# LayerNorm outputs transposed once in float32 instead of twice in split form, in a fused attention and ternary feed-forward kernel

## The chip, the cores and the metric

The kernel runs on one core of a Trainium2 chip. The metric is the device time of one execution in microseconds (us). Before the change it is 1569.74 us, the median of three runs (1567.95 to 1573.29).

The engines are named as in the profile: PE (TensorE, matrix multiplication; PEld are its weight loads), DVE (VectorE), ACT (ScalarE), POOL (GpSimd) and SP (SyncE, which here only issues DMAs). Each engine works through its own queue in order and waits on semaphores for the others.

## The reference

The input x has 8 batches of 1024 tokens with 256 features. The reference is a sandwich of two sublayers, each with a LayerNorm (without weights) ahead of it and one behind it:

```python
x = x + _layernorm(_L0_attn_ref(_layernorm(x), Wq, Wk, Wv, Wo))
x = x + _layernorm(_L0_ffn_ref(_layernorm(x), weight, alpha, bias))
```

```python
q, k, v = x @ Wq, x @ Wk, x @ Wv      # 16 query heads, 4 key/value heads of 16
q, k = _rope(q), _rope(k)
p = softmax(einsum('bhqd,bhkd->bhqk', q, k) / sqrt(256))
o = einsum('bhqk,bhkd->bhqd', p, v)
return o @ Wo
...
w = ternary_quantize(weight) * alpha   # entries -1, 0, 1
return einsum('bsd,od->bso', input, w) + bias
```

All of it is float32.

## The kernel before

**Tiling.** The tokens are cut into 16 units of 512 (`NU`), two per batch; a unit is four tiles of 128 tokens, handled as two pairs p = 0 and 1. For each unit there are three streams of work.

- The *projection* (class `Project`): LayerNorm of x (`begin`), transposing the normalised pairs so that features lie on the partitions (`x`), key/value product (`kv_and_dram`, then `kt` and `v`), query product (`q`), and the way of the queries through DRAM into the stacked layout `q_st` (`q_to_dram`, `stack_queries`).
- The *attention scores*: PE computes scores twice. The first time (`sm`, line 608) DVE takes row maxima (line 621). The maxima go through a small transpose (`pm`, line 655) and a DMA (`q_st<-ml`, line 671) into extra rows of the queries, so that the second scores (`se`, line 680) come out shifted and ACT can take the exponential directly (line 701). The exponentials are multiplied by the values (`av`, line 721), and `av_out` sends the sums to DRAM (`d_av<-avsb`, line 742).
- The *tail* (class `Tail`): fetch of the sums, division by the softmax denominator, output product `attn`, LayerNorm and residual (`stats_a`), second LayerNorm (`stats_x`), transposing (`x` or `xw`), ternary product `ffn`, last LayerNorm and residual (`stats_f`), store.

**Split products.** A product in full float32 is made from fp32r parts: each operand is split into a high part (rounded to fp32r) and a low part (the rest), and `product` (line 297) adds up high x high, high x low and low x high. Where an operand has to be transposed first, there are two ways in the kernel before:

- `transposed` (line 262) is called once for the high part and once for the low part. Both parts were made before, by POOL (`split_hi`, line 155: a multiplication by one that writes fp32r; `split_lo`, line 161: a subtraction). Each call is four 128x128 fp32r transposes on PE into one bank of PSUM and one copy by ACT (line 271).
- `transposed_split` (line 274) transposes the float32 values themselves, four 128x128 fp32 transposes into one bank (line 279). ACT copies the bank to SBUF once (line 284), and POOL makes both parts from that copy. Only the tails of units 12, 13 and 14 use it (`W_PARTS`, line 999, step name `xw`).

In the projections of units 3 to 15 the high and low parts `xs` take the buffer named `hl` in the pool `qkp`, which has one buffer; the split queries `hlq`, which four DMAs read, take the same one.

**Order.** A unit has 32 steps (`SPU`); a step is four exponent scores. `P_PARTS`, `T_PARTS` and their variants for the first and last units say at which step each part falls due; a projection starts at step 26 of one unit and ends at step 62, which is step 30 of the next; a tail runs during the unit after its own. On PE, ACT and DVE the order is written out (`manual_schedule`); for POOL and SP the recording layer orders the instructions. From exponent score 40 on the written order comes from a planner (`plan`, `Course`, `group`): it searches over *groups*, each of some `se` and `sm` scores, then parts that are due, then a piece of `av`. PSUM banks limit it: exponent scores and parts share three banks (`ps_e`), so a group holds three exponent scores and no part that needs a bank, or two and one such part. The planner works with costs on PE and ACT, in ns, in `WORK` (line 1199), and `banked` (line 1098) lists which parts need a bank.

Of the kernel before, what the change touches and what calls it, by code (L numbers as in the profile page):

```python
# [8 lines left out]
F32 = mybir.dt.float32  # L9
F32R = mybir.dt.float32r  # L10
# [6 lines left out]
P = 128  # L17
# [11 lines left out]
def kernel(  # L29
# [29 lines left out]
    nc = tc.nc  # L59
# [4 lines left out]
    ND = D // P  # L64
    NK = S // P
    UPB = S // UQ
    NU = B * UPB
# [8 lines left out]
    work = ctx.enter_context(tc.tile_pool(name="work", bufs=2))  # L76
# [78 lines left out]
    def split_hi(eng, hi, src):  # L155
        if eng is nc.gpsimd:
            eng.tensor_scalar(hi, src, 1.0, 0.0, ALU.mult, ALU.add)  # L157
        else:
            nc.scalar.copy(hi, src)

    def split_lo(eng, lo, src, hi):
        eng.tensor_tensor(lo, src, hi.bitcast(F32), ALU.subtract)  # L162

    def split(eng, hi, lo, src, hi_eng=None):

        split_hi(hi_eng or eng, hi, src)
        split_lo(eng, lo, src, hi)
# [25 lines left out]
    ffn = {}  # L193
# [68 lines left out]
    def transposed(src, tag, name, copy=nc.scalar.copy):  # L262

        pt = psum([P, ND, 2 * P], f"pt_{name}", F32R)
        for t in range(2):
            for c in range(ND):
                nc.tensor.transpose(  # L267
                    pt[:, c, t * P : (t + 1) * P], src[:, t, c * P : (c + 1) * P], ident_r
                )
        dst = work.tile([P, ND, 2 * P], F32R, tag=tag, name=name, bufs=2 if tag[0] == "x" else 1)  # L270
        copy(dst, pt.bitcast(F32))
        return dst

    def transposed_split(src, tag, name):

        pt = psum([P, ND, 2 * P], f"pt_{name}")
        for t in range(2):
            for c in range(ND):
                nc.tensor.transpose(
                    pt[:, c, t * P : (t + 1) * P], src[:, t, c * P : (c + 1) * P], ident  # L280
                )

        whole = work.tile([P, ND, 2 * P], F32R, tag="xt0", name=name).bitcast(F32)
        nc.scalar.copy(whole, pt)
        parts = [
            work.tile([P, ND, 2 * P], F32R, tag=f"{tag}{l}", name=f"{name}_{l}", bufs=1)
            for l in range(2)
        ]
        split(nc.gpsimd, *parts, whole)
        return parts  # L290

    TERMS = ((0, 0), (0, 1), (1, 0))
# [30 lines left out]
    class Project:  # L323
# [3 lines left out]
        def __init__(self, u, eng):  # L327
            self.u, self.eng = u, eng
            self.b, self.half = divmod(u, UPB)
            self.xt, self.sc, self.hl = {}, {}, {}  # L330
            self.q_rot = None
            if u not in (1, 2):
                xn = qkp.tile([P, UT, D], F32, tag="xn", name=f"xn_{u}", bufs=2)
                xs = qkp.tile([P, 2, UT, D], F32R, tag="hl", name=f"xs_{u}")
                self.xn = [xn[:, 2 * p : 2 * p + 2, :] for p in range(2)]
                self.xs = [[xs[:, l, 2 * p : 2 * p + 2, :] for l in range(2)] for p in range(2)]
            else:
# [21 lines left out]
        def begin(self, p):  # L359
            self.stats(p)  # L360
            self.norm(p)
            self.hi(p)
            self.lo(p)

        def x(self, p, l):
            self.xt[p, l] = transposed(self.xs[p][l], f"xt{l}", f"xt{l}_{self.u}_{p}")

        def kv(self, p):

# [375 lines left out]
    class Tail:  # L745
# [65 lines left out]
                self.copy(p)(hl[:, 0], self.on[p])  # L811
            split_lo(self.eng(p), hl[:, 1], self.on[p], hl[:, 0])

        def x(self, p, l):
            self.xt[p, l] = transposed(self.hl[p][:, l], f"ot{l}", f"ot{l}_{self.u}_{p}")

        def xw(self, p):
            self.xt[p, 0], self.xt[p, 1] = transposed_split(self.on[p], "ot", f"ot_{self.u}_{p}")

# [20 lines left out]
        def stats_x(self, p):  # L840
            self.sc[p] = ln_stats(self.x1[p])
            self.norm(p)
            if not NU - 4 <= self.u < NU - 1:
                self.split(p)

        def stats_f(self, p):
# [25 lines left out]
    class LastTail(Tail):  # L872
# [55 lines left out]
        x = o  # L928
# [42 lines left out]
    def load(u):  # L971
# [2 lines left out]


    P_PARTS = (
        (26, "begin", 0), (33, "x", 0, 0), (34, "x", 0, 1), (37, "begin", 1), (43, "x", 1, 0),
        (45, "x", 1, 1), (49, "kv_and_dram"), (51, "q", 0), (54, "kt"), (53, "v"), (55, "q", 1),
        (62, "q_to_dram"),
    )  # L980
    L_PARTS = (
# [5 lines left out]
    T_PARTS = (  # L987
        (1, "fetch"), (7, "invert"), (8, "scale", 0), (9, "scale", 1), (12, "attn", 0),
        (15, "attn", 1), (15, "stats_a", 0), (17, "stats_a", 1), (19, "stats_x", 0),
        (23, "stats_x", 1), (24, "x", 0, 0), (25, "x", 0, 1), (26, "ffn", 0), (27, "x", 1, 0),  # L990
        (29, "x", 1, 1), (31, "ffn", 1), (31, "stats_f", 0), (33, "stats_f", 1),
    )


    P_SECOND = (26, 33, 34, 37, 43, 45, 49, 51, 52, 53, 55, 57)
    T_FIRST = (6, 8, 11, 12, 14, 16, 16, 17, 20, 23, 24, 25, 26, 27, 29, 31, 31, 33)
    P_FIRST = (47, 51, 52, 54, 57, 58, 59, 60, 62, 61, 63, 64)

    W_PARTS = (
        (1, "fetch"), (7, "invert"), (8, "scale", 0), (9, "scale", 1), (12, "attn", 0),  # L1000
        (15, "attn", 1), (15, "stats_a", 0), (17, "stats_a", 1), (19, "stats_x", 0),
        (22, "xw", 0), (23, "stats_x", 1), (26, "ffn", 0), (27, "xw", 1), (31, "ffn", 1),
        (31, "stats_f", 0), (33, "stats_f", 1),
    )
    T_LAST = (1, 3, 4, 5, 9, 10, 11, 14, 17, 19, 20, 22, 25, 27, 24, 28)

    warm = []
# [76 lines left out]
    for u in range(NU - 1):  # L1084
        start = SPU * (u + 1)
        at(start + 1, begin_tail, u)
        parts = T_PARTS if u < NU - 4 else W_PARTS
# [82 lines left out]
    def window(s):  # L1170
# [26 lines left out]


    WORK = {
        "x": (460, 477), "xw": (460, 477), "q": (1620, 477), "kv_and_dram": (1620, 477),  # L1200
        "v": (330, 270), "attn": (1620, 477), "ffn": (1125, 560), "n": (460, 477),
        "o": (460, 477),
    }
# [345 lines left out]
```

## Time and profile before

| what | value |
|---|---|
| median of 3 runs | 1569.74 us |
| the profiled execution | 1569.75 us |
| its span, first to last instruction | 1568.0 us |
| mean granted PE clock | 0.996 |
| fp32r transposes, lines 267 (`pt_xt`, `pt_ot`) | 480 |
| fp32 transposes, line 279 (`pt_ot`) | 24 |
| ACT copies behind them, lines 271 and 284 | 118 + 6, mean 592 to 614 ns |
| POOL, high part of a pair, line 157 (`xs`, `hl`, `ot`) | 87, mean 619 to 623 ns |
| POOL, low part of a pair, line 162 (`xs`, `hl`, `ot`) | 89, mean 1273 to 1285 ns |
| DVE row maxima, line 621 | 605 of 128x1024 (1219 ns), 838 of 128x512 (683 ns) |

In a group line a name left of the arrow is what is written and names right of it are what is read; shapes are partitions by elements. The counts of lines 157 and 162 hold the splits of the attention output (`hl` in `scale`) too. A PE instruction's duration overlaps that of its neighbours, because matmuls are pipelined; its cost to the queue is read from the start of one piece of work to the start of the next.

### The profile page before, as it was taken

How to read it: one execution, taken by the hardware profiler on the slowest of the kernel's cores; microseconds unless marked ns; L12 is line 12 of the kernel's file. 1: busy time of each engine (PE TensorE's matmuls, PEld its weight loads, DVE VectorE, ACT ScalarE, POOL GpSimd, SP SyncE). 2: the span in 40 equal slices, each digit the busy share in tenths (PEclk: the TensorE clock that was granted, in tenths of full speed). 3: DMA queues.
4: the chain of work that ended last, by engine and by line, in shares of the span. 5: the costliest groups of instructions: out<-in, count | busy, mean ns of one | idle time of the engine just before them, and what ended most of it. 6: DMA issues, size and time to landing. Idle time of an engine off the chain costs nothing.

```text
span 1568.0 us, 35573 instructions
## 1 busy us (share of the span) xinstructions
PE 1527.8 (97%) x13854; PEld 779.0 (50%) x13854; DVE 1411.6 (90%) x2172; ACT 1268.8 (81%) x2473; POOL 835.8 (53%) x1239
## 2 busy tenths in 40 slices
PE   8999999999999999999999999999999999999997
PEld 6544454554545455454544545455454544444444
DVE  7888898999899999999999899999999999999965
ACT  4677878888887888888888888888888787878874
POOL 6553466383845647474573756547385543323354
PEclk9999999999999999999999999999999999999999
DMA  5161525133161513415152251514225151321100
GB/s 145 55 96 49 112 73 112 63 82 83 61 130 46 97 61 87 96 59 117 54 93 70 78 107 59 113 49 88 63 68 110 45 99 45 61 58 36 43 15 27
DMA packets 86071, 117.86 MB, mean 75 GB/s; under 512 B 12088, under 2 KB 50808, under 8 KB 85752
## 3 DMA queue, kind: packets, MB, share of 16 engines
q1 hardware_dynamic: 85904, 115.60, 31.9%
q8 instruction: 109, 1.79, 0.5%
q14 instruction: 58, 0.48, 0.1%
HBM read 68.65 MB, written 45.88 MB: 73 GB/s over the span
## 4 chain that ended last, share of the span: by engine, by line
PE 88%; DVE 5%; POOL 2%; DMA 2%; ACT 1%; issue 1%; SPq 0%; POOLq 0%; ACTq 0%; DVEq 0%
PE av L721 32%; PE se L680 27%; PE sm L608 13%; DVE mx L621 4%; PE pa L301 3%; PE pq L301 3%; PE pf L301 2%; PE pt_xt L267 2%; PE pt_ot L267 2%; PE pkv L301 1%; DMA q_st<-ml 1%; ACT e L701 1%; PE pm L655 1%; POOL lnsc L242 0%; DMA x<-in_L_attn_x 0%
## 5 line engine op out<-in xcount | busy, mean ns | idle before, releaser
L621 DVE TENSOR_REDUCE mx<-sm 128x1 f32<-128x512 f32 (+1 forms) x1443 | 1237.4, 908 | 112.7 <-PE sm L608 78.9
L701 ACT ACTIVATE e<-se 128x512 f32<-128x512 f32 x1996 | 1059.4, 600 | 161.5 <-PE sm L608 96.2
L608 PE MATMUL sm<-k_st,q_st 64*128 64x512 f32 x2048 | 692.1, 445 | 6.4 <-DVE mx L621 5.9
L680 PE MATMUL se<-q_st,k_st 64*128 64x512 f32 x2048 | 685.5, 439 | 9.9 <-DMA q_st<-ml 3.8
L721 PE MATMUL av<-e,v_aug 128*32 128x128 f32 (+3 forms) x7736 | 604.3, 402 | 0.0
L680 PEld LDWEIGHTS se<-q_st,k_st 64*128 64x128 f32 x2048 | 322.0, 184 | 421.4 <-ACT e L701 326.7
L608 PEld LDWEIGHTS sm<-k_st,q_st 64*128 64x128 f32 x2048 | 315.4, 184 | 40.6 <-DVE mx L621 24.1
L721 PEld LDWEIGHTS av<-e,v_aug 128*32 128x32 f32 x7736 | 167.6, 108 | 191.2 <-issue 143.5
L241 POOL TENSOR_SCALAR lnsc<-mv 128x2 f32<-128x2 f32 (+1 forms) x134 | 25.7, 192 | 355.5 <-DVE mv L239 349.8
L795 POOL TENSOR_TENSOR xn<-xn,a 128x512 f32<-128x512 f32 x30 | 38.4, 1281 | 124.4 <-DMA a<-d_rec 104.9
L242 POOL TENSOR_TENSOR lnsc<-lnsc,mhalf 128x2 f32<-128x2 f32 (+1 forms) x134 | 92.3, 689 | 0.9
L162 POOL TENSOR_TENSOR hl<-xn,hl 128x512 fp32r<-128x512 f32 x54 | 68.7, 1285 | 0.0
L253 POOL TENSOR_SCALAR xn<-x,lnsc 128x256 f32<-128x256 f32 x116 | 64.9, 568 | 3.4
L860 POOL TENSOR_TENSOR a<-a,bias_bc 128x512 f32<-128x512 f32 x30 | 38.4, 1282 | 45.8 <-ACT a L859 45.8
L157 POOL TENSOR_SCALAR xs<-xn 128x512 fp32r<-128x512 f32 x27 | 16.8, 623 | 68.2 <-DMA dq<-hlq 66.9
L301 PE MATMUL pq<-xt,wqkvh 128*128 128x256 f32 x256 | 44.1, 294 | 3.9 <-DVE ml L664 3.5
L315 POOL TENSOR_TENSOR t<-q_rot,sin_q_sb 128x512 f32<-128x512 f32 x31 | 40.2, 1298 | 12.6 <-ACT q_rot L457 11.6
L301 PE MATMUL pa<-woh,hl 128*128 128x256 f32 x240 | 46.3, 295 | 0.0
L237 DVE BATCH_NORM_STATS2 bnst<-x 128x6 f32<-128x256 f32 x124 | 45.8, 410 | 0.1
L237 DVE BATCH_NORM_STATS2 bnst<-a 128x6 f32<-128x256 f32 x120 | 44.6, 413 | 0.1
L301 PE MATMUL pf<-wt,ot 128*128 128x256 f32 x256 | 38.6, 292 | 5.2 <-ACT e L701 5.2
L825 ACT COPY a<-pa 128x512 f32<-128x512 f32 x30 | 17.6, 587 | 29.2 <-issue 29.2
(163 smaller groups left out, 1316.2 us busy)
## 6 DMA issues: line engine op xcount, KB each, us to landing
q_st<-dq SPq DMA_DIRECT2D x90, 256.0 KB
dq<-hlq SPq DMA_DIRECT2D x60, 256.0 KB
d_av<-avsb SPq DMA_DIRECT2D x60, 256.0 KB
x<-in_L_attn_x SPq DMA_DIRECT2D x15, 512.0 KB
xn<-d_av SPq DMA_DIRECT2D x30, 256.0 KB
a<-d_rec SPq DMA_DIRECT2D x30, 256.0 KB
xr<-in_L_attn_x SPq DMA_DIRECT2D x15, 512.0 KB
out_x<-a SPq DMA_DIRECT2D x30, 256.0 KB
```

Of the source, the lines that this page charges most:

```text
L162: eng.tensor_tensor(lo, src, hi.bitcast(F32), ALU.subtract)
L237: nc.vector.bn_stats(st[:, t, :], src[:, t, :])
L242: nc.gpsimd.tensor_tensor(sc[:, 1, :], sc[:, 1, :], mhalf[:, :n], ALU.pow)
L253: eng.tensor_scalar(dst[:, t, :], src[:, t, :], sc[:, 0, t : t + 1] if eng is nc.gpsimd else mv[:, t, 0:1], sc[:, 1, t : t + 1], ALU.add i ...
L267: nc.tensor.transpose(pt[:, c, t * P : (t + 1) * P], src[:, t, c * P : (c + 1) * P], ident_r)
L301: nc.tensor.matmul(out, chunk(left[i], c), chunk(right[j], c), start=(k == 0), stop=(k == len(steps) - 1),)
L315: eng.tensor_tensor(dst, x, table.unsqueeze(1).to_broadcast(list(x.shape)), ALU.mult)
L608: scores = nc.tensor.matmul(self.sm[:, part, :], queries[rows], k_st[(u // UPB) % 3][rows, r2, self.ch * 512 : (self.ch + 1) * 512], start ...
L621: self.early = nc.vector.tensor_reduce(self.out[:, new], self.sm[:, new, :], AX.X, ALU.max).ins
L680: nc.tensor.matmul(sc if len(queries.shape) == 2 else sc.rearrange("p (j t) -> p j t", j=G), k_st[(i // G // UPB) % 3][rows, r2, kt * P : ...
L701: nc.scalar.activation(e, sc, AF.Exp, scale=1.0 / D**0.5)
L721: nc.tensor.matmul(av_ps[0][32 * r : 32 * r + 32, lo:hi], va[:, kt, r, :], es[i * NK + kt, r // 2, r % 2][:, lo:hi], start=(kt == 0 and lo ...
```

## The change

For the projections of units 3 to 15 and for the tails of units 0 to 14 a pair is transposed once in float32, and the two parts are made behind the transpose. `transposed_split` itself changes too: ACT now reads the bank twice, once writing the high part (rounded to fp32r) and once writing the whole value, and the whole value overwrites the normalised tile that has just been transposed. POOL makes only the low part. `begin` no longer splits, the projections of units 3 to 15 no longer allocate `xs`, and the tail's `stats_x` splits only in the last unit. The step tables have one `xw` per pair where they had two `x`, and the planner's cost of `xw` on ACT is doubled. The projections of units 0 to 2 and the tail of unit 15 stay as they were.

```diff
@@ transposed_split
-        whole = work.tile([P, ND, 2 * P], F32R, tag="xt0", name=name).bitcast(F32)
-        nc.scalar.copy(whole, pt)
         parts = [
-            work.tile([P, ND, 2 * P], F32R, tag=f"{tag}{l}", name=f"{name}_{l}", bufs=1)
+            work.tile(
+                [P, ND, 2 * P], F32R, tag=f"{tag}{l}", name=f"{name}_{l}",
+                bufs=2 if tag[0] == "x" else 1,
+            )
             for l in range(2)
         ]
-        split(nc.gpsimd, *parts, whole)
+        whole = src.rearrange("p (c t) d -> p c (t d)", c=ND)
+        nc.scalar.copy(parts[0], pt)
+        nc.scalar.copy(whole, pt)
+        split_lo(nc.gpsimd, parts[1], whole, parts[0])
         return parts
@@ Project
+            if u == 0:
                 xs = qkp.tile([P, 2, UT, D], F32R, tag="hl", name=f"xs_{u}")
...
         def begin(self, p):
             self.stats(p)
             self.norm(p)
-            self.hi(p)
-            self.lo(p)
...
+        def xw(self, p):
+            self.xt[p, 0], self.xt[p, 1] = transposed_split(self.xn[p], "xt", f"xt_{self.u}_{p}")
@@ Tail
-        def x(self, p, l):
-            self.xt[p, l] = transposed(self.hl[p][:, l], f"ot{l}", f"ot{l}_{self.u}_{p}")
...
-            if not NU - 4 <= self.u < NU - 1:
+            if self.u == NU - 1:
                 self.split(p)
@@ the step tables
-        (26, "begin", 0), (33, "x", 0, 0), (34, "x", 0, 1), (37, "begin", 1), (43, "x", 1, 0),
-        (45, "x", 1, 1), (49, "kv_and_dram"), (51, "q", 0), (54, "kt"), (53, "v"), (55, "q", 1),
+        (26, "begin", 0), (33, "xw", 0), (37, "begin", 1), (43, "xw", 1),
+        (49, "kv_and_dram"), (51, "q", 0), (54, "kt"), (53, "v"), (55, "q", 1),
...
-        (23, "stats_x", 1), (24, "x", 0, 0), (25, "x", 0, 1), (26, "ffn", 0), (27, "x", 1, 0),
-        (29, "x", 1, 1), (31, "ffn", 1), (31, "stats_f", 0), (33, "stats_f", 1),
+        (22, "xw", 0), (23, "stats_x", 1), (26, "ffn", 0), (27, "xw", 1), (31, "ffn", 1),
+        (31, "stats_f", 0), (33, "stats_f", 1),
...
@@ WORK
-        "x": (460, 477), "xw": (460, 477), "q": (1620, 477), "kv_and_dram": (1620, 477),
+        "x": (460, 477), "xw": (460, 954), "q": (1620, 477), "kv_and_dram": (1620, 477),
```

The tables for the first units (`P_FIRST`, `P_SECOND`, `T_FIRST`) are shortened in the same way, and `W_PARTS` goes, since `T_PARTS` now has its steps.

More of the change, by code (lines that the diff above doesn't have):

```diff
@@ L333, in __init__ @@
                 xn = qkp.tile([P, UT, D], F32, tag="xn", name=f"xn_{u}", bufs=2)
+                self.xn = [xn[:, 2 * p : 2 * p + 2, :] for p in range(2)]
+            if u == 0:
                 xs = qkp.tile([P, 2, UT, D], F32R, tag="hl", name=f"xs_{u}")
-                self.xn = [xn[:, 2 * p : 2 * p + 2, :] for p in range(2)]
                 self.xs = [[xs[:, l, 2 * p : 2 * p + 2, :] for l in range(2)] for p in range(2)]
-            else:
+            elif u < 3:
                 self.xn = [
@@ L989 @@
         (15, "attn", 1), (15, "stats_a", 0), (17, "stats_a", 1), (19, "stats_x", 0),
-        (23, "stats_x", 1), (24, "x", 0, 0), (25, "x", 0, 1), (26, "ffn", 0), (27, "x", 1, 0),
-        (29, "x", 1, 1), (31, "ffn", 1), (31, "stats_f", 0), (33, "stats_f", 1),
[L992 to L1001, printed above, removed]
         (22, "xw", 0), (23, "stats_x", 1), (26, "ffn", 0), (27, "xw", 1), (31, "ffn", 1),
@@ L1004 @@
     )
+    P_SECOND = (26, 33, 37, 43, 49, 51, 52, 53, 55, 57)
+    T_FIRST = (6, 8, 11, 12, 14, 16, 16, 17, 20, 22, 23, 26, 27, 31, 31, 33)
+    P_FIRST = (47, 51, 54, 57, 59, 60, 62, 61, 63, 64)
     T_LAST = (1, 3, 4, 5, 9, 10, 11, 14, 17, 19, 20, 22, 25, 27, 24, 28)
@@ L1086 @@
         at(start + 1, begin_tail, u)
-        parts = T_PARTS if u < NU - 4 else W_PARTS
+        parts = T_PARTS
         steps = {0: T_FIRST, NU - 2: T_LAST}.get(u, [k for k, *_ in parts])
```

## The prediction

> **What bounds the kernel now.** First the page: engine totals, and the chain of work that ended last.
>
> ```profile
> span 1568.0 us, 35573 instructions
> PE 1527.8 (97%) x13854; PEld 779.0 (50%) x13854; DVE 1411.6 (90%) x2172; ACT 1268.8 (81%) x2473; POOL 835.8 (53%) x1239
> PE 88%; DVE 5%; POOL 2%; DMA 2%; ACT 1%; issue 1%; SPq 0%; POOLq 0%; ACTq 0%; DVEq 0%
> ```
>
> TensorE (PE) sets the end, but VectorE (DVE) is 90% busy and does not come far behind. Then the busy time by stretch, for units 10, 13 and 14, each cut at every 128th exponent score. The columns are length, then PE, weight loads, DVE, ACT and POOL busy with counts, then granted clock and DMA.
>
> ```profile
> 982.80:1075.70 92.90, 91.99 (x874) 46.94 (x870) 86.22 (x133) 78.21 (x153) 53.47 (x79) 1.00 0.35 81
> 1261.90:1349.50 87.60, 84.77 (x765) 39.60 (x761) 80.10 (x122) 72.77 (x143) 31.32 (x47) 1.00 0.32 70
> 1349.50:1437.30 87.80, 86.25 (x786) 40.43 (x782) 83.82 (x121) 73.20 (x143) 30.54 (x46) 1.00 0.26 57
> ```
>
> Units 2 to 12 are alike (92.5 to 93.2 us). Units 13 and 14 have no projection beside them, and in the kernel before they already hold the single fp32 transpose, so they show what less PE work brings. They lack two query products (1.7 us each, 869.03 to about 870.7), one key/value product (1.7), the value transposes (0.4), four groups of xt transposes (1.9) and 0.7 of the ot ones: 8.1 us, and with five groups fewer (0.15 each, below) 8.9. They are only 5.2 us shorter, so 58% came through. The clock is 1.00 throughout and plays no part.
>
> **PE: fewer transposes.** Now the timeline, first a group of four fp32r transposes, then one of four fp32 ones (start, length).
>
> ```profile
> 800.40 0.54 PE L267 MATMUL pt_ot<-ident_r,hl 128*128 128x128 f32 x4
> 800.87 0.64 PE L721 MATMUL av<-e,v_aug 128*32 128x128 f32 x16
> 801.24 0.59 ACT L271 CAST ot<-pt_ot 128x512 fp32r<-128x512 f32 x1
> 802.02 0.39 PE L608 MATMUL sm<-k_st,q_st 64*128 64x512 f32 x1
> ```
> ```profile
> 1341.23 0.66 PE L279 MATMUL pt_ot<-ident,xn 128*128 128x128 f32 x4
> 1341.82 0.16 PEld L721 LDWEIGHTS av<-e,v_aug 128*32 128x32 f32 x8 [0.17 <-issue]
> ```
>
> Busy times overlap, so I take start to the next work: 0.47 us in fp32r, 0.59 in fp32. A pair of transposes (high, low) becomes one: 2 x 0.47 - 0.59 = 0.35. There are 26 pairs in the projections of units 3 to 15 and 24 in the tails of units 0 to 11 (tails 12 to 14 are fp32 already): 50 x 0.35 = **-17.5 us**.
> The Trainium skill, FP8 and Floating Point Precision, TensorE Precision Notes, speaks against this: true fp32 takes four passes through the array. By that rule a group would cost 4 x 0.47 = 1.88 us, each pair would lose 0.94, and the kernel would gain 47 us of PE work. The rows of L279 contradict it for transposes (0.59).
>
> **PE: fewer groups.** A group with a step that needs a score bank holds two exponent scores instead of three, so fewer such steps mean fewer groups. In the order of the built instructions the groups of scores fall from 789 to 777, and a steady unit from 50 to 49. The price of a group: one with two scores of each kind, two columns of av and a row-maximum transpose lasts 1.45 us (866.53 to 867.98), 1.17 without the 0.28 of that transpose; three such carry what two groups of three carry, which last 1.68 each (801.44 to 803.12): (3.51 - 3.36) = 0.15. 12 x 0.15 = **-1.8 us**. Bounds: nothing, and 0.36 (the idle time of the weight loads inside such a group), -4.3.
>
> **What is given back, 1: the query-shift DMA.** Once a unit, at step 8, the second block's scores need rows that SP sends late. SP's queue and that place on PE:
>
> ```profile
> 908.38 0.34 SPq L742 DMA_DIRECT2D d_av<-avsb  x1
> 919.17 0.65 SPq L772 DMA_DIRECT2D xn<-d_av  x1
> 921.20 1.41 SPq L671 DMA_DIRECT2D q_st<-ml  x2
> 1109.96 0.47 PE L680 MATMUL se<-q_st,k_st 64*128 64x512 f32 x1 [0.52 <-DMA q_st<-ml]
> ```
>
> The shift (L671) is computed some 5 us before it is issued; it stands in SP's queue behind the fetch L772, which waits 9 us for d_av to land behind the six query loads issued from step 0 on. PE begins that block at 923.93, 2.0 us after the second shift was issued; other units wait 0.2 to 0.5 for it. So steps 0 to 8 already last as long as this chain, and what the change saves there is lost: the projection's first pair and its group, 0.35 + 0.15, in 12 units, **+6.0**. Bounds 0 (DMAs land earlier) and +6.0.
>
> **Given back, 2: the second copy.** ScalarE still copies twice per pair, but both now come from one bank. Consecutive copies start 0.50 apart. Above, the copy ends at 801.83 and the bank's next user starts about 802.02 beside the last L608: 0.18 of room. It grows by 0.12 (longer transposes; the copy started late behind two exponentials anyway) and by 0.18 where three columns of av stand behind the transposes instead of two, as after most of them in the new order. So 0 to 0.2 is exposed where a full group of three follows, which the new order has 26 times; elsewhere the bank's next user comes later. 26 x 0.1 = **+2.6**. Bounds: 0, and 0.32 at all 56 (50 new, 6 in tails 12 to 14, which had one copy before) = +18. ACT's six copies more (3.6 us) lie in its 19% of idle time otherwise.
>
> **Given back, 3: VectorE.** Its reductions are the same, in less time, and 22 more of them are split (1443 to 1465 instructions): two halves cost 2 x 0.683 against 1.219, so 22 x 0.15 = 3.2 us of work. Units 13 and 14 lost 42% of their cut, where DVE is 91 to 95% busy; a steady unit goes from 93% by far less. Of the cut that is left, 17.5 + 1.8 - 6.0 = 13.3, I take a quarter: **+3.3**. Bounds 0 and 42%, +5.6.
>
> **At nothing: POOL, SP, buffers.** POOL loses 56 operations (26 + 24 + 6 high halves of 0.62 each, the low ones stay) and its 66.9 us of waiting for the query DMA (L157 behind dq<-hlq), since the projection's split no longer shares a buffer with hlq. Neither ends a PE wait now. The low half is now made after the transpose (1.28 us): PE needs it at step 26 or 31 in a tail, four steps or some 11 us after the transposes, and six steps later in a projection, which covers it; without cover it would be 1.28 per pair, 64 us. SP issues the same DMAs in the same order. Where the normalised tile itself must be early is the second rival.
>
> Sum: -17.5 - 1.8 + 6.0 + 2.6 + 3.3 = -7.4 us. The profiled execution took 1569.75 (span 1568.0 and 1.75 around it), the median of the runs is 1569.74: **1562.3 us**.
>
> **Rivals.** What this kernel's measurement can tell from no change is about 0.3%, 4.7 us.
> *Absorbed.* The DMA chain takes its 6.0, DVE its 5.6, and the copy 0.2 at 26 places (5.2): -19.3 + 16.8 = -2.5, **1567.3**. For it: units 13 and 14. Against: there the cut was nine times a steady unit's, and DVE was left without relief by longer groups.
> *All of it comes through.* The order keeps the copies covered and the DMAs move with PE: -19.3 and a larger price of a group, **1549 to 1552**. For it: PE is 99% busy in unit 10. Against: the waits on L671.
> *PE waits for POOL at the tail's first transposes.* Slower. The fp32 transposes of a tail read the norm directly, and in the new order stand ahead of the second query product, not behind it.
>
> ```profile
> 876.09 1.29 POOL L315 TENSOR_TENSOR q_rot<-q_rot,cos_q_sb 128x512 f32<-128x512 f32 x1
> 877.37 1.10 POOL L253 TENSOR_SCALAR xn<-x,lnsc 128x256 f32<-128x256 f32 x2
> 884.12 0.54 PE L267 MATMUL pt_ot<-ident_r,hl 128*128 128x128 f32 x4
> ```
>
> POOL has no idle time from 869.73 on; the norm ends at 878.47, 10.5 us after the group with the first query product began (867.98). In the new order the transposes come 3.0 + 1.7 + 1.5 + 1.7 + 1.7 and 0.8 of scores, 10.4 us, after it. The key chain ahead of the norm starts some 0.8 earlier there (three groups of 5.6 us instead of 4.8 between key/value and query product), so I reckon 0.7 us of room. If one POOL operation more (1.3 us) stood in front, PE would lose 0.6, if two, 1.9 in each of 12 units, with all later work of the PE queue behind it: -7.4 + 23 = +16, **1585**. It decides from (7.4 + 4.7) / 12 = 1.0 us of wait on.
>
> **Chances.** Forecast 0.42, absorbed 0.25, all through 0.15, POOL wait 0.18. The first and third are faster by over 0.3%: 0.57; same 0.25; slower 0.18. The forecast's own range is 1557 to 1565; with half of the rivals' ends, **1551 to 1577**.
>
> **What would show it.** Steady units of about 92.1 us instead of 92.9; pt_ot and pt_xt groups of 0.59 from start to next work; a longer wait of L680's line for q_st<-ml at step 8; POOL's wait for dq<-hlq gone; PE idle before the transposes at most a few tenths. I am wrong if PE waits there for xn, if steady units are below 91.6 (no give-back) or if the score after a transpose group waits on the copy by more than 0.2.

## The result, and the profile after

| | before | after |
|---|---|---|
| median of the runs | 1569.04 us (4 runs, 1567.95 to 1573.29) | 1595.32 us (4 runs, 1593.15 to 1597.91) |
| ratio to the kernel before | | 1.0163, 95% interval 1.0137 to 1.0189 |
| span of the profiled execution, clock | 1568.0 us, 0.996 | 1591.8 us, 0.994 |
| units 0 and 1 together | 196.3 us | 208.4 us |
| a unit of 2 to 12, mean | 92.82 us | 93.75 us |
| units 13 to 15 together | 267.8 us | 270.6 us |

The change made the kernel slower by 26 us; 1562 was forecast. A unit is counted here, as in the prediction, from its first exponent score to that of the next; unit 15 is counted to its last score. The page of the kernel after, engine totals and the chain of work that ended last:

```profile
span 1591.8 us, 34919 instructions
PE 1525.1 (96%) x13518; PEld 761.3 (48%) x13518; DVE 1414.8 (89%) x2194; ACT 1272.3 (80%) x2479; POOL 804.8 (51%) x1183
PE 80%; DVE 6%; DMA 5%; ACT 3%; POOL 2%; issue 2%; SPq 1%; POOLq 0%; DVEq 0%; ACTq 0%
```

PE's own share of the chain fell from 88 to 80%; DMA rose from 2 to 5, ACT from 1 to 3, DVE from 5 to 6. So most of the lost time is waiting, and it is spread over several engines; in unit 1 the granted clock adds to it (below). The busy time of units 10, 13 and 14, in the columns of the prediction:

```profile
1017.20:1110.40 93.20, 91.35 (x849) 45.60 (x846) 86.45 (x136) 78.12 (x153) 51.27 (x74) 1.00 0.33 81
1297.50:1385.60 88.10, 85.25 (x759) 38.99 (x756) 83.11 (x119) 73.60 (x144) 29.38 (x44) 1.00 0.27 61
1385.60:1474.40 88.80, 86.35 (x778) 39.93 (x774) 84.00 (x121) 74.19 (x145) 29.39 (x44) 1.00 0.27 57
```

PE is 0.64 us less busy in unit 10 and idle 0.94 us longer. Units 13 and 14, whose transposes were in float32 before as well, are longer by 0.5 and 1.0 us: something other than the number of transposes changed there.

The table of waits, the lines that matter (us in total, times, longest), after and then before:

```profile
PEld sm L614 <- DVE mx L627: 35.6, 96, 1.0
PE se L686 <- DMA q_st<-ml: 13.0, 9, 6.9
PEld pt_ot L279 <- POOL xn L253: 3.0, 3, 2.3
PE pt_ot L279 <- POOL xn L253: 2.0, 1, 2.0
```
```profile
PEld sm L608 <- DVE mx L621: 24.1, 59, 1.0
PE se L680 <- DMA q_st<-ml: 3.8, 6, 1.4
```

Scores wait more for row maxima and for the row shift. The prediction's slower rival, PE waiting for POOL's norm ahead of the tail's transposes, is nearly absent: 3 us of the weight loads' waits, and one PE wait of 2.0 us, in unit 1.

**SP's queue in a steady unit.** Unit 9 starts at 922.5. SP's queue around it, from the timeline (start, length), and below it the query copy and the six loads of the kernel before, where unit 9 starts at 903.8:

```profile
914.19 1.37 SPq L677 DMA_DIRECT2D q_st<-ml  x2
915.66 4.68 SPq L496 DMA_DIRECT2D dq<-hlq  x4
920.89 4.81 SPq L570 DMA_DIRECT2D q_st<-dq  x6
...
928.33 0.34 SPq L748 DMA_DIRECT2D d_av<-avsb  x1
...
939.77 0.65 SPq L778 DMA_DIRECT2D xn<-d_av  x1
...
941.80 1.43 SPq L677 DMA_DIRECT2D q_st<-ml  x2
```
```profile
893.42 4.69 SPq L490 DMA_DIRECT2D dq<-hlq  x4
902.17 2.68 SPq L564 DMA_DIRECT2D q_st<-dq  x6
```

The last row-maximum transpose of a unit now stands behind score step 29.0 (27.75 before), and the query copy `dq<-hlq` is recorded behind that shift. So the copy starts 6.8 us ahead of the unit, where it was 10.4; the last of the six loads behind it is issued at +2.8 instead of +0.6, d_av goes at 5.8 instead of 4.6, and the shift that step 8 needs at 19.3 instead of 17.4 after the unit's start. PE's timeline shows what that costs, in unit 9 and, first, in unit 1:

```profile
186.79 0.76 PE L686 MATMUL se<-q_st,k_st 64*128 64x512 f32 x1 [6.94 <-DMA q_st<-ml]
...
944.82 0.47 PE L686 MATMUL se<-q_st,k_st 64*128 64x512 f32 x1 [1.50 <-DMA q_st<-ml]
```

Unit 1 starts at 158.7 and has a cause of its own. The recording layer put the query copy of unit 3 ahead of the shift, between two parts of the loads for unit 2 (that it did so because POOL, relieved of the splits, has these queries ready earlier is argued, not tested):

```profile
166.07 1.85 SPq L570 DMA_DIRECT2D q_st<-dq  x4
168.02 0.37 SPq L748 DMA_DIRECT2D d_av<-avsb  x1
168.49 3.13 SPq L496 DMA_DIRECT2D dq<-hlq  x4
172.49 2.32 SPq L570 DMA_DIRECT2D q_st<-dq  x2
...
177.74 1.86 SPq L677 DMA_DIRECT2D q_st<-ml  x2
```

The shift was computed at 173.9 and issued at 177.7. Step 8 comes 28.1 us after the unit's start (22.0 before); the unit takes 107.5 us (97.0).

Not all of these 10.5 us is waiting. Unit 1 before and after, then two stretches of it after, in the columns of the prediction:

```profile
157.50:254.50 97.00, 93.43 (x876) 47.29 (x872) 87.13 (x128) 78.00 (x153) 54.26 (x75) 1.00 0.40 92
```
```profile
158.70:266.20 107.50, 96.90 (x825) 47.21 (x824) 86.10 (x124) 78.69 (x153) 51.91 (x72) 0.94 0.32 84
182.90:193.10 10.20, 6.31 (x40) 3.12 (x42) 4.20 (x5) 3.72 (x7) 0.00 (x0) 0.50 0.38 111
237.60:241.00 3.40, 3.40 (x14) 1.27 (x16) 0.10 (x1) 1.21 (x3) 2.40 (x2) 0.50 0.08 22
```

PE has fewer matmuls in this unit (825 for 876) and is 3.5 us longer busy. For 10.2 us from within the wait of 6.94, and for 3.4 us behind the wait of 2.0 for the norm (it ends at 237.0), the granted clock was 0.50. The prediction's "plays no part" holds for the steady units, whose clock is 1.00 here too.

### The profile page after: what moved, and what is told of

Read it like the earlier page. It is cut to its first block, busy times and chain, and to the rows that moved or that the text cites. A ratio compares the mean times of both kernels' runs of the same rounds, so it can differ in the third digit from the quotient of the medians.

```text
span 1591.8 us, 34919 instructions
## 1 busy us (share of the span) xinstructions
PE 1525.1 (96%) x13518; PEld 761.3 (48%) x13518; DVE 1414.8 (89%) x2194; ACT 1272.3 (80%) x2479; POOL 804.8 (51%) x1183
## 4 chain that ended last, share of the span: by engine, by line
PE 80%; DVE 6%; DMA 5%; ACT 3%; POOL 2%; issue 2%; SPq 1%; POOLq 0%; DVEq 0%; ACTq 0%
PE av L727 30%; PE se L686 26%; PE sm L614 11%; DVE mx L627 5%; PE pq L305 3%; PE pa L305 2%; ACT e L707 2%; PE pf L305 2%; DMA q_st<-ml 2%; PE pkv L305 1%; PE pt_ot L279 1%; PE pt_xt L279 1%; PE pm L661 1%; DMA d_av<-avsb 1%; DMA den<-d_av 1%
## 5 line engine op out<-in xcount | busy, mean ns | idle before, releaser
L686 PE MATMUL se<-q_st,k_st 64*128 64x512 f32 x2048 | 695.9, 441 | 26.0 <-DMA q_st<-ml 13.0
L614 PE MATMUL sm<-k_st,q_st 64*128 64x512 f32 x2048 | 703.6, 449 | 9.2 <-DVE mx L627 8.1
L162 POOL TENSOR_TENSOR ot<-xn,ot 128x512 fp32r<-128x512 f32 x30 | 38.7, 1289 | 45.0 <-ACT xn L292 45.0
L162 POOL TENSOR_TENSOR xt<-xn,xt 128x512 fp32r<-128x512 f32 x26 | 33.4, 1283 | 46.6 <-ACT xn L292 46.6
L305 PEld LDWEIGHTS pa<-woh,hl 128*128 128x128 f32 x240 | 34.7, 190 | 15.3 <-issue 9.0
```

The costliest lines, as they stand in the source:

```text
L305: nc.tensor.matmul(out, chunk(left[i], c), chunk(right[j], c), start=(k == 0), stop=(k == len(steps) - 1),)
L614: scores = nc.tensor.matmul(self.sm[:, part, :], queries[rows], k_st[(u // UPB) % 3][rows, r2, self.ch * 512 : (self.ch + 1) * 512], start ...
L686: nc.tensor.matmul(sc if len(queries.shape) == 2 else sc.rearrange("p (j t) -> p j t", j=G), k_st[(i // G // UPB) % 3][rows, r2, kt * P : ...
```

## The experiments

The theories, under the letters that the expectations use: **A**, late query copies on SP's queue; **B**, the second copy on ACT holds a PSUM bank and delays exponentials; **C**, VectorE has no room for shorter units; **D**, the row-maximum transpose keeps its bank too long; **P**, the planner's redrawn order costs the time and not the work; **T**, the rival to P, the transposes and copies themselves. All orders are those of the kernel after unless said otherwise. "Group" lengths run from the start of a group's first score to the start of the next group's, as means over units 4 to 11.

### First four: the query copies and the second copy

a1 takes the query copy of each unit from 5 on out of its place behind the newest shift:

```diff
-            behind = [behind_latest] if u > 4 and p[0] in ("kt", "q_to_dram") else []
+            behind = [behind_latest] if u > 4 and p[0] == "kt" else []
```

> The changed kernel, with the query DMAs of a projection (dq<-hlq) no longer ordered behind the latest row-maximum shift on SP's queue; the order on PE, ACT and DVE is the same. Theory A (late query DMAs): in the changed kernel these DMAs start 6.8 us before step 0 of a steady unit instead of 10.4 before, collide with the loads q_st<-dq, and make PE wait at step 8. Then they start some 3 us earlier here, step 8 comes about 20.4 us after step 0 instead of 21.4, and the time falls by some 10 us to about 1585. Theory B (the second copy of ScalarE holds up the next scores) and theory C (VectorE has no room for shorter units): no change, 1595.

1588.41 us, ratio 1.0129 [1.0108, 1.0150]. The copy starts 13 us ahead of the unit, units 2 to 12 fall from 93.75 to 93.21 us.

a2 holds the copy of unit 3 back, behind the shift of unit 1:

```diff
-    P_FIRST = (47, 51, 54, 57, 59, 60, 62, 61, 63, 64)
+    P_FIRST = (47, 51, 54, 57, 59, 60, 62, 61, 63, 76)
...
-            behind = [behind_latest] if u > 4 and p[0] in ("kt", "q_to_dram") else []
+            behind = [behind_latest] if u > 4 and p[0] in ("kt", "q_to_dram") or u == 3 and p[0] == "q_to_dram" else []
```

> The changed kernel, with the query DMAs of unit 3 moved from step 0 to step 12 of unit 1, behind the shift and the fetch; the order on PE, ACT and DVE is the same. In the changed kernel they stand between two parts of the loads q_st<-dq, and unit 1 takes 107.5 us instead of 97.0. Theory A: step 8 of unit 1 comes at 22 us instead of 28, and the tail of unit 0 follows earlier, so the time falls by 6 to 10 us to 1585 to 1589. Theories B and C: no change, 1595.

1588.81 us, 1.0124 [1.0107, 1.0141]; unit 1 falls from 107.5 to 104.0.

a3 goes back to one copy per pair of transposes:

```diff
-        nc.scalar.copy(parts[0], pt)
         nc.scalar.copy(whole, pt)
-        split_lo(nc.gpsimd, parts[1], whole, parts[0])
+        split(nc.gpsimd, *parts, whole)
```

> The changed kernel, with one copy by ScalarE (the whole value) and both parts made by POOL from it, in the same written order. Theory B: each of the 56 pairs gives back 0.2 to 0.4 us, so 1573 to 1584. Theory A: the waits lie elsewhere, 1593 to 1597; POOL's high half (0.62 us) lies in its idle time. Theory C: 1595.

1594.48 us, 1.0154 [1.0137, 1.0171]: nothing gained. The group behind the first transposes is 0.10 us shorter and the one behind that 0.11 longer. In this order B costs nothing that can be measured.

a5 has the edits of a1 and a2 together.

> Both edits of the query DMAs together (a steady unit's free of the shift, unit 3's moved to step 12 of unit 1). Theory A: the two add up, 1573 to 1580, close to the kernel before. Theories B and C: 1595.

1585.18 us, 1.0103 [1.0088, 1.0118]. A is worth 10.1 us of the 26, less than A's forecast (1573 to 1580). Steps 6 to 8 of a unit still take 5.8 us (4.8 before), and steps 8 to 32 take 72.4 us as in the kernel before, though three pairs are transposed there once instead of twice. Sixteen us stayed open.

### Second four: the order, the bank, VectorE

b1 is the kernel **before** with one constant of the planner's search changed, and no work:

```diff
-    LOW, HIGH, MARGIN, EXPS, WIDTH = 44, 62, 16, 12, 50
+    LOW, HIGH, MARGIN, EXPS, WIDTH = 44, 62, 16, 12, 40
```

> The kernel before with one constant of its planner changed (it keeps 40 candidate courses a step where it kept 50): the same work, the same transposes and copies, another written order (791 planned groups for 789; in a steady unit the row-maximum transpose that the next block waits for comes after score step 28.25 instead of 27.75, and a transpose group follows it instead of a feed-forward group). Theory P (what is left of the loss is the order that the planner wrote, not the work that the change moves): the steady unit grows from 92.8 us by 0.3 to 1.2, and the time by 4 to 15, to 1574 to 1585. Rival T (the loss belongs to the transposes, the copies and the fewer groups of the change): within 3 us of the kernel before, 1567 to 1573.

1593.87 us, 1.0159 [1.0140, 1.0177], as slow as the kernel after and beyond P's forecast (1574 to 1585). Its page and its unit 10:

```profile
span 1590.2 us, 35420 instructions
...
PE 83%; DVE 5%; POOL 5%; DMA 3%; ACT 2%; issue 1%; SPq 0%; POOLq 0%; ACTq 0%; DVEq 0%
```
```profile
1010.30:1104.50 94.20, 92.43 (x865) 46.37 (x860) 86.26 (x133) 78.45 (x153) 53.33 (x78) 1.00 0.35 80
```

DVE's and ACT's busy times are those of the kernel before (86.22 and 78.21), and so is the work; the same scores in another written order take 94.2 us instead of 92.9. An order alone can cost what the change cost. That does not say yet that it is what the change cost.

b2 is a5 with the low part of the row maxima first in its group:

```diff
+        take_low()
         q = m = 0
         state = Course(s, av)
```

> The changed kernel with both repairs of the query copies, and the low part of the row maxima (ml) recorded as the first thing of the group after its transpose instead of after that group's first score, on VectorE ahead of that score's reduction; TensorE's and ScalarE's orders as before. Theory D (the transpose pm keeps one of three PSUM banks until ml has been read, so the group after it runs on two: over their contents those four groups of a steady unit take 2.1 us in the changed kernel, 0.6 in the kernel before): the third score or the part in them no longer waits for the first exponent, 0.5 us less in two of the four, 0.9 to 1.2 us less a unit, some 1573 (1570 to 1577). Rival (that wait only covers ScalarE or VectorE, which are as late without it): 1583 to 1588, the four groups as long as before.

1573.41 us, 1.0026 [1.0015, 1.0038]: 11.8 us less than a5, D's number. The timeline of a5 at the group behind the third row-maximum transpose of a unit:

```profile
1067.13 0.50 PE L686 MATMUL se<-q_st,k_st 64*128 64x512 f32 x1
1067.18 0.24 ACT L663 CAST mh<-pm 32x128 fp32r<-32x128 f32 x1
...
1067.66 1.09 ACT L707 ACTIVATE e<-se 128x512 f32<-128x512 f32 x2 [0.24 <-PE sm L614]
...
1067.70 0.69 DVE L627 TENSOR_REDUCE mx<-sm 128x1 f32<-128x512 f32 x1 [0.16 <-PE sm L614]
1068.31 0.33 DVE L670 SCALAR_TENSOR_TENSOR ml<-mh,low,pm 32x128 fp32r<-32x128 f32 x1
...
1068.31 0.74 PE L305 MATMUL pq<-xt,wqkvh 128*128 128x256 f32 x4 [0.46 <-ACT e L707]
```

The transposed maxima stay in one of three banks until DVE has made `ml` from them. `ml` stands behind a reduction of the group that follows, so the query product `pq` takes the bank of that group's first exponent and starts only when that has been read. With `ml` first (b2), the same place:

```profile
1057.27 0.50 PE L686 MATMUL se<-q_st,k_st 64*128 64x512 f32 x1
1057.33 0.24 ACT L663 CAST mh<-pm 32x128 fp32r<-32x128 f32 x1
...
1057.61 0.33 DVE L670 SCALAR_TENSOR_TENSOR ml<-mh,low,pm 32x128 fp32r<-32x128 f32 x1
...
1057.99 0.53 PEld L305 LDWEIGHTS pq<-xt,wqkvh 128*128 128x128 f32 x4 [0.31 <-DVE ml L670]
1057.99 0.74 PE L305 MATMUL pq<-xt,wqkvh 128*128 128x256 f32 x4
```

`pq` now follows `ml` and no longer an exponent. From the group's first score to `pq` it is 0.72 us instead of 1.18. Two of the four groups behind such transposes got 0.47 and 0.46 us shorter (2.40 to 1.93, 3.16 to 2.70), the other two did not change. Units 2 to 12 take 92.41 us, 0.41 less than in the kernel before (0.29 less than in c3, told below, which is the kernel before with the same edit): in the steady units of this repaired order part of the saving arrives. The planner's model frees this bank after the ACT copy; it knows nothing of `ml`.

b3 is a5 with the search constant at 70.

> The changed kernel with both repairs of the query copies and its planner's constant at 70 courses for 50: the transposes and copies of the change in another written order (779 groups for 777; the last row-maximum transpose after score step 27.0 instead of 29.0, and 13.0 and 20.0 for 13.5 and 20.75). Theory P: the row shift is early again, the step 8 of a unit comes before 20.4 us after its step 0, the steady unit takes 91.6 to 92.6 us, the time is 1566 to 1578. Rival T: the order is worth nothing, steady units stay at 93.2 and the time at 1583 to 1588.

1589.91 us, 1.0138 [1.0106, 1.0170], above both forecasts. The miss of theory P: the early row maxima brought step 8 to 20.7 us, not below 20.4, and the transposes now wait for POOL's norm (5.5 us in 8 waits; the longest 2.0). An order that looks better by one sign is another draw.

b4 is a5 with half of each row-maximum reduction; half of the keys are left out of the row maxima:

```diff
-                self.out[:, new], self.sm[:, new, :], AX.X, ALU.max
+                self.out[:, new], self.sm[:, new, :256], AX.X, ALU.max
```

> The changed kernel with both repairs of the query copies, where VectorE's reductions of the row maxima read 256 of each bank's 512 columns: half of the keys are left out of the row maxima, and some 0.25 us of each reduction of one bank; all orders as they were. Theory C (VectorE, busy at every score, has no room for a unit with fewer fillers): the waits of TensorE for mx are gone and the steady unit falls by over 1 us, to some 92.0, the time to 1570 or below. Theory D or P: VectorE is only late where the written order makes it, the groups after the row-maximum transposes keep most of their 2.1 us, the time falls by less than 8, to 1577 to 1585.

1548.58 us, 0.9865 [0.9847, 0.9884]; units 2 to 12 take 91.61. VectorE does set the pace. Whether it sets it more than in the kernel before needs c4.

### Third four: the change in the old order

c1 gives the planner the old tables and costs (three of the edits are shown, the rest are alike), and does the new work in the first of each two old places:

```diff
+        def y(self, p, l):
+            if l == 0:
+                self.xw(p)
...
-        (26, "begin", 0), (33, "xw", 0), (37, "begin", 1), (43, "xw", 1),
-        (49, "kv_and_dram"), (51, "q", 0), (54, "kt"), (53, "v"), (55, "q", 1),
+        (26, "begin", 0), (33, "y", 0, 0), (34, "y", 0, 1), (37, "begin", 1), (43, "y", 1, 0),
+        (45, "y", 1, 1), (49, "kv_and_dram"), (51, "q", 0), (54, "kt"), (53, "v"), (55, "q", 1),
...
-        "x": (460, 477), "xw": (460, 954), "q": (1620, 477), "kv_and_dram": (1620, 477),
+        "x": (460, 477), "y": (460, 477), "xw": (460, 477), "q": (1620, 477), "kv_and_dram": (1620, 477),
```

> The change in the written order of the kernel before: transposes in float32, the second copy on ScalarE, no split of units 3 on, but the planner is given the old table of parts and costs (the first part of each old pair does the float32 transpose and both copies, the second is left as an empty place that the planner still counts), so that all 789 groups, every score, reduction and row-maximum transpose stand as in the kernel before, and 50 groups lack a transpose of 0.47 us. Theory P (the loss is the order that the planner wrote): the steady unit goes from 92.8 us to 91.4 to 92.4, step 8 stays at 20.4 after step 0, the row-maximum transpose that sends the shift stays at 27.75; the time is 1552 to 1563, below the kernel before. Rival T (the transposes, the copies or the norm that now stands straight ahead of the transposes cost the time): 1569 or more, up to 1595.

1580.60 us, 1.0069 [1.0049, 1.0088]. P's forecast (1552 to 1563) is missed; the time lies in the range of rival T (1569 to 1595). It is below the kernel after, so the order counts, but 12.0 us above the kernel before in the same batch (1568.60), so the order is not all of it. Unit 1 has 5.4 us of that (102.4 against 97.0), with a wait of 5.36 us for the row shift. Since all 50 groups of a unit correspond, their lengths can be set side by side (us; the last two columns are runs told below):

| behind step | what the group holds | before | c1 | d2 |
|---|---|---|---|---|
| 2.75 | transposes of pair 1, now in float32 | 1.70 | 1.82 | 1.82 |
| 3.50 | three scores | 1.68 | 2.03 | 1.68 |
| 4.00 | its transposes are gone | 1.49 | 1.02 | 1.02 |
| 4.50, 5.25 | maxima transpose; three scores | 3.60 | 3.65 | 3.95 |
| 13.00 | transposes of pair 2, now in float32 | 1.49 | 1.61 | 1.61 |
| 13.50 | two scores, maxima transpose | 1.67 | 2.03 | 1.66 |
| 14.50 | its transposes are gone | 2.47 | 2.00 | 2.00 |
| 15.25 | three scores | 1.69 | 2.16 | 2.16 |
| 26.00 | transposes of pair 3, now in float32 | 1.70 | 1.82 | 1.82 |
| 26.50 | its transposes are gone | 1.95 | 1.47 | 1.47 |
| 27.25 | three scores | 1.67 | 2.10 | 2.10 |
| 28.75 | transposes of pair 4, now in float32 | 1.71 | 1.82 | 1.82 |
| 29.50 | three scores | 1.68 | 2.02 | 1.68 |
| 30.75 | its transposes are gone | 1.71 | 1.24 | 1.24 |

Each float32 group costs 0.12 more and each removed one 0.47 less, as forecast. But the group behind the float32 transposes is 0.35 longer in three places, and the group behind a removed one 0.42 to 0.47 longer in two. The first kind, in c1's timeline (the bank's two copies, then the weight load of the next group's third score):

```profile
1015.91 0.59 ACT L291 CAST xt<-pt_xt 128x512 fp32r<-128x512 f32 x1
...
1016.38 0.62 ACT L292 COPY xn<-pt_xt 128x512 f32<-128x512 f32 x1
...
1017.05 0.18 PEld L690 LDWEIGHTS se<-q_st,k_st 64*128 64x128 f32 x1 [0.52 <-ACT xn L292]
```

and the second, at step 15:

```profile
1047.38 4.15 DVE L631 TENSOR_REDUCE mx<-sm 128x2 f32<-128x1024 f32 x5 [0.25 <-PE sm L618]
```
```profile
1049.79 0.18 PEld L618 LDWEIGHTS sm<-k_st,q_st 64*128 64x128 f32 x1 [0.42 <-DVE mx L631]
```

DVE works five reductions on end there. The removed transposes had given it time; without them PE arrives early and waits. So in c1 no pair keeps its 0.35: pairs 1 and 4 give it back in the first way, pair 3 in the second, pair 2 in both.

c2 adds b2's edit to c1.

> As the kernel of the old order with the changed transposes, and the low part of the row maxima (ml) recorded as the first thing of the group after its transpose, on VectorE ahead of that group's first reduction. Theory D (the bank of the row-maximum transpose, kept until ml has been read): the four groups after those transposes take 0.6 us a unit over their contents in the kernel before; half of it at most goes, 0 to 0.3 us a unit, 0 to 5 us below the kernel of the old order, some 1555. Rival (VectorE is then late for the scores): no gain or 1 to 4 us above it.

1582.81 us, 1.0076 [1.0056, 1.0096]: no gain, the rival's answer.

c3 is the kernel before with b2's edit.

> The kernel before with only this edit: the low part of the row maxima (ml) recorded first in the group after its transpose. Theory D: the edit gave 11.8 us to the changed kernel because its plan had the stall (2.1 us a unit behind the four row-maximum transposes); the kernel before has 0.6 us there, so 0 to 5 us, 1564 to 1569. Rival (the edit is worth the same whatever the order): 1557.

1570.33 us, 1.0008 [0.9996, 1.0021]: no difference. D's stall belongs to the redrawn order: in the old one PE's weight loads wait for `ml` itself at two of the four places, as long with the edit as without (0.4 us at step 5.25, 0.6 at the query product), and the group of the ternary product gets 0.06 us shorter.

c4 is the kernel before with b4's edit.

> The kernel before with VectorE's reductions of the row maxima reading 256 of each bank's 512 columns: half of the keys are left out of the row maxima; all orders as they were. The same edit took 36.6 us from the changed kernel with the repaired copies (1548.6). Theory C (VectorE covers what the change saves on TensorE): the kernel before gains less, as TensorE has more to do there, and stands 8 to 15 us above, at 1556 to 1564. Theory P: VectorE's time is worth as much to both, the kernel before falls by some 30 to 36 us to 1533 to 1540, below the changed one.

1535.09 us, 0.9777 [0.9753, 0.9801]. This is P's forecast: the halving takes 33.5 us here and 36.6 from a5, nearly the same. Units 2 to 12 are then equal (91.55 against 91.61), and most of the 13.5 us between the two lies in unit 1 (93.4 against 104.5, where PE waits 4.17 us for the row shift and the clock is 0.95). But b4 still has D's stall: its two groups take 2.40 and 3.17 us, together 0.94 a unit more than in b2. So the equal units do not show that the change gains nothing where VectorE has time to spare; b2 with the halved reductions was not run.

### Last six: what is left in the old order

d1 is c1 with the copy of unit 3 held back, as in a2.

> The change in the old order, and the query copy of unit 3 (dq) held behind the row shift of unit 1 on SyncE's queue as the kernel before had it by chance. Theory A for unit 1: its step 8 goes from 26.3 back to 22 us after step 0 and the unit from 102.4 to 97 or 98, the time from 1580.6 to 1574 to 1577. Rival: the shift is late for another reason, 1579 to 1582.

1574.98 us, 1.0039 [1.0025, 1.0053]; unit 1 goes from 102.4 to 100.0. That is 5.6 us in the medians and 2.4 in unit 1 of the profiled execution, which was the slowest of nine (1580.85).

d2 is d1 with a3's single copy.

> As the kernel of the old order with the copy of unit 3 held back, and one copy on ScalarE per pair of transposes instead of two: ScalarE copies the whole once, GpSimd makes the high and the low part from it. Theory B (the second copy keeps the bank and ScalarE for 0.6 us, and the next group waits): the group behind the first transposes loses its 0.35 us in three or four places of a unit, 1.0 to 1.4 us a unit, the steady unit 92.0 and the time 12 to 17 below d1, 1558 to 1564. Rival C (VectorE's reductions set the pace of these groups; in the new order the same edit gave nothing): within 4 us of d1.

1569.52 us, 1.0000 [0.9983, 1.0018]. 5.5 us, between the two forecasts: the three places behind the float32 transposes lose exactly their 0.35 (column d2 above), while the 0.47 and 0.42 at steps 15.25 and 27.25 stay, and at steps 4.50 and 5.25 the gain of pair 1 is now given back as well. Pair 4 keeps its 0.35, of which the group of the ternary product takes back 0.17 (2.67 to 2.84). Both theories hold, each at its own places.

d3 and d4 are redrawn orders of the changed kernel with a5's and b2's repairs (`WIDTH` 40, and `"xw": (460, 477)` in `WORK`).

> The changed kernel with both repairs of the query copies, the low part first, and the planner's constant at 40 courses for 50: another order (768 groups for 777; three-score groups or full groups behind the row-maximum transposes). Theories D and P: with the bank stall gone an order with fewer groups has steady units of 91.6 to 92.4 us, the time 1562 to 1573. Rival: an order is a draw, and this one is no better than the others, 1575 to 1595.

> The changed kernel with both repairs of the query copies, the low part first, and the planner charging one copy of 477 ns on ScalarE for a transpose pair instead of two: another order (771 groups). Theories D and P: steady units of 91.6 to 92.4 us, the time 1562 to 1573. Rival: a draw like the others, 1575 to 1595.

1577.29 us, 1.0059 [1.0040, 1.0077], and 1576.09 us, 1.0054 [1.0036, 1.0071]: fewer groups (768, 771) and no gain over b2. In d4 every other unit takes 91.85 us and the next 93.6. Draws, as the rival said.

f1 is d2 with the copy of unit 3 directly behind the third shift of unit 1 (76 becomes 80 in `P_FIRST`).

> The change in the old order with one copy on ScalarE per pair, and the query copy of unit 3 directly behind the third row shift of unit 1, as in the kernel before. Unit 1 goes from 99.6 to 97 or 98 us and the time from 1569.5 to 1566 to 1568; steady units stay at 92.5 to 92.7, since nothing was taken from VectorE. Rival: unit 1 is long for another reason, 1569 to 1572.

1568.76 us, 1.0001 [0.9983, 1.0018], beside a kernel before of 1570.05 in that batch. Unit 1 takes 95.2 us. With order, copies and queue as good as before, the change is worth nothing that can be measured in this order.

f2 is f1 with b4's halved reductions.

> The same kernel with VectorE's reductions of the row maxima reading 256 of each bank's 512 columns (half of the keys left out of the row maxima). Theory C (VectorE was the cover): the groups behind the removed transposes no longer grow by 0.42 to 0.47 us, the steady unit falls from 91.5 us (kernel before, halved) to 90.1 to 90.7 and the time stands 10 to 18 below the halved kernel before (1535.1), at 1517 to 1525. Rival (ScalarE, or the planned order itself, is the cover): 1531 to 1538.

1553.85 us (1547.68 to 1562.47), 0.9911 [0.9879, 0.9942]. The time is far from C's forecast, and above the rival's. Beside c4, group by group, C is nevertheless seen where it was claimed: the groups behind the removed transposes no longer grow (step 15.25: 1.69 and 1.68 us; 27.25: 1.67 and 1.66), and a unit is 1.26 us shorter than c4's up to step 27.75. There it loses 2.2 us at the ternary product and 0.65 at the transposes behind it. The table of waits says for what, and the line below it has the clock (0.50) around the end of the longest of these waits, at 876.8:

```profile
PE pf L304 <- POOL ot L157: 10.8, 10, 3.3
PE pf L304 <- POOL ot L162: 8.9, 11, 0.9
```
```profile
875.40:882.20 6.80, 4.84 (x24) 3.27 (x24) 0.85 (x2) 1.68 (x3) 6.03 (x9) 0.50 0.17 48
```

PE waited 1.1 us there in d2 and not at all in c4. POOL, which with one copy makes high and low part behind the transpose, is the next in line. The clock is a second part of the loss: the five runs have a mean of 0.984 to 0.989, c4's 0.996 to 1.000; the clock of units 8 and 9 is 0.96, and the transposes behind the ternary product take 1.82 us in the four of units 4 to 11 without such a stretch and 2.47 to 3.21 in the others. Without the loss in these two groups a unit would be some 1.5 us shorter than c4's (an estimate from the same group means), near C's forecast for a unit (90.1 to 90.7 against 91.5). But that gain was never seen in a time, so what the change would be worth with room on VectorE and POOL both stays open.

## Why the prediction was wrong

- **PE's transposes, -17.5.** Right in size: +0.12 for a float32 group and -0.47 for a removed one, in every place of the table. The Trainium skill (FP8 and Floating Point Precision, TensorE Precision Notes) has four passes for float32; for these transposes that would have been some 1.4 us more a group (an estimate from 0.47). The runs show 0.12, and they decide.
- **Fewer groups, -1.8.** The count was right, its worth not seen: d3 and d4 have nine and six groups fewer still and are no faster than b2. What a group costs depends on what stands behind what. This term is the step that failed first: the prediction took the new order as the old one with 12 groups fewer. b1 shows that redrawing the order with no change of work can cost 25 us, and b2 finds 11.8 us of the 26 in one property of the drawn order, a bank held until `ml`.
- **The query-shift DMA, +6.0, and "SP issues the same DMAs in the same order" at nothing.** Absorbed saving was allowed for, a later chain was not: the upper bound of +6.0 assumed that the DMAs stay where they are in time. They did not, because one stands behind a shift that the new order makes 1.25 steps later, and another came ahead of a shift. Undoing both gives 10.1 us (a5). The prediction also had the clock at 1.00 throughout, and unit 1 got 0.94.
- **The second copy, +2.6 (0 to 18).** Right in mechanism and within the bounds: 0.8 us in the new order, not told from nothing, and 5.5 us in the old one, at three places of 0.35, where the prediction took 0 to 0.2 for one.
- **VectorE, +3.3 (0 to 5.6).** The mis-sized term. It was sized as a quarter of what was left, from units 13 and 14, where 42% of a cut was lost. In the old order, once copies and queue are repaired (d2, f1), nothing of the 17.5 arrives in the time; two of four pairs are given back whole in the very next group behind the removed transposes, and a third in the two groups behind them (steps 4.50 and 5.25). The page said 90% busy; the question that was not asked is whether the groups that lose work are among those where DVE is late.
- **POOL and the norm.** The slower rival (1585) came near the time for the wrong reason: PE waited once for the norm there, 2.0 us, and its weight loads 3 us in all. POOL's wait for the query copy did go, as forecast; that this is what put unit 3's copy ahead of the shift is likely, but was not tested.
- **What the sum comes to.** 1595.3 - 10.1 (A) - 11.8 (D) = 1573.4, measured in b2. The 4.4 us by which that is above the kernel before are a balance. In the profiled executions, 2.5 us apart, units 0 and 1 of b2 are 5.5 us longer than before, units 13 to 15 2.0 longer, and units 2 to 12 together 4.5 shorter. Unit 1 takes 101.3 us against 97.0; it waits 2.16 us for POOL's norm at its tail's first transposes, which is the slower rival at one place, and its clock is 0.97. The other road, old order, -5.6 (copy of unit 3), -5.5 (second copy), ends at 1569.5, and there the saving is covered by VectorE at three of four pairs, seen group by group in d2 and, without it, in f2.

## What to carry to other kernels

Where a planner writes the order, price the redraw before the edit: change one search constant on the old kernel and look at the spread (here 25 us, where the forecast hung on 7), and judge an edit in the old order as well as in its own. Work taken off an engine that leads by a few per cent over another (97 against 90% busy) counted here only in the groups where the other is not the one that is late; look there, not at the share of the span. A transfer held behind "the newest" of something moves whenever that something does, however far it stands from the edit. And where an experiment makes an engine wait, read its granted clock beside the waits before the difference is put down to the waits alone.

## What the hardware showed that was not expected

Four 128x128 transposes in float32 cost PE 0.12 us more than in fp32r (1.82 against 1.70 for the whole group), not a multiple. The groups' lengths repeat almost to the hundredth from unit to unit (with the waits in them: 2.16 us at step 15.25 in both c1 and d2), so a stall of 0.35 us can be read off a table of means; the groups at step 8, which a DMA ends, vary more (0.99 to 1.62 us before, 1.22 to 2.78 after), and so does the ternary product where it waits for POOL. A wait of PE for some microseconds cost more than itself: from within a wait of 6.94 us in unit 1 on, the granted clock was 0.50 for 10.2 us, and PE was 3.5 us longer busy in that unit with fewer matmuls.
